# Attention and spiking feed-forward on one core: the last division through TensorE, later biases, and an order without random draws

## The chip, the core and the metric

One core of a Trainium2 chip runs the whole kernel in one launch. The metric is device microseconds of that core; lower is better. The engines are TensorE (PE, matrix products, with its weight loads shown apart as PEld), VectorE (DVE), ScalarE (ACT), GpSimd (POOL) and SyncE (SP, which issues nearly all DMAs here). Each engine takes its own instructions strictly in order, and waits on semaphores for the others.

## The reference, cut to what matters

The input x is [16, 1024, 256] in f32 (16 batches, 1024 tokens, 256 features). 16 heads have 16 features each; the feed-forward is 1024 wide.

```python
xn = layernorm(x)
Q, K, V = (xn @ W.T + b for each of q, k, v)        # split into 16 heads of 16
Q, K = rope(Q), rope(K)
scores = Q @ K.T / 4, causal mask
attn = softmax(scores) @ V                          # per head
a = concat(attn) @ Wo.T + bo
h = square(relu(xn @ W_fc.T)); y = h @ W_proj.T
f = number of spikes in 5 steps of a leaky neuron driven by y, over 5
out = x + a + f
```

## The kernel before, in words

**Units.** The attention works in 64 units: batch b, group g of four heads (`NG` = 4). For each unit `largest` (L785) first forms all causal scores (PE, L797) and takes each query's maximum on DVE (L813 for whole blocks, L831 for blocks on the diagonal). `placed` (L849) turns these maxima round on PE (L858), and SP writes them as two extra rows into the unit's query tile (L875). `weighted` (L904) then forms the scores again, transposed and with the maximum taken off by those rows (PE, L914), exponentiates them on ACT into "w" tiles (L975), masks the diagonal blocks on POOL (L932) and multiplies with the values (PE, L941, f32, four heads side by side in column quarters of the array). The values carry a column of constants beside each head's 16, so that the product has the sum of the exponentials in row 16 of each head's 32.

**The division.** Queries go in two halves `qb` of 512. When a half of a unit is done, its product is copied from PSUM to `avT` (L406, ACT, sometimes DVE at L412) and stored to DRAM (`av_dram`, L991). When two units (eight heads) are there, SP loads the sums (L1000) and the values (L1006) in a denser layout, DVE takes the reciprocals (L1014), SP stores them (L1017) and loads them spread over the 16 rows of each head (`inv`, `spread`, L949). POOL multiplies (L1023), ACT casts to f16 (L1025) and POOL keeps the remainder as a second f16 (L1028). These pairs of f16 are the `attn` tiles (128 rows for eight heads) that `projected` (L1033) multiplies with `wo_hi` and `wo_lo` (L599); DVE adds the product to the output tile (L1049) and SP stores that (L1052). A product in f32 precision from f16 parts is three f16 products (`three`, L596).

**Everything else.** `norms` (layer norm, transposes by DMA, L636), `rotated` (q and k with rope; on DVE in batch 0, on POOL in all others; stored to the DRAM scratch `scr`, L696 and L700), `values` (L738), and the feed-forward `forward` (L1072: `wfc` and `wproj` products at L599, L1106 to L1117 on ACT and POOL, the spikes on DVE at L1128). The x tile of the output is scaled on ACT (L1144) and gets the output bias `bo_sb` on POOL (L1146).

**The order.** All this is not issued as it is written. Each piece is an `op` with an engine, a cost, and a time `when` at which it is due; `Plan.order` (L199) plays the program through with these costs and writes the order in which each engine gets its instructions. An op may start up to a window (93 us of the plan's time unless given) before it is due, once what it reads is there and its tiles and PSUM banks are free. Buffers of one tag are handed out in turn: the next one waits until the oldest is free. The tag "w" has five buffers, "qkhl" (the f16 pairs of the rotated q and k) two. Each op's cost in that play is varied by up to 3% with a random generator whose seed is changed every 70 us of the plan; the seeds are the list `DRAWN` (L112 to L115, used at L273 to L276 and L328).

**The start.** `load_small` (L530) issues five DMAs on SP: wo in two parts, bv in two parts, bo. It is due at `SMALL` = -20 us of the plan, with a window of 10 us. From these come `wo_hi` and `wo_lo`, `bv_wide` (L550), a bias product on PE (L555) and the output bias (`biases`, L561).

```python
    op("sp", dma(5), SMALL, load_small, [], ["small", wo_stage], size=1400.0, window=10e3)
```

Of the kernel before, what the change touches and what calls it, by code (L numbers as in the profile page):

```python
# [4 lines left out]

# [1 line left out]

# [49 lines left out]
def least_values():  # L57
# [3 lines left out]
    for n in range(1, NUM_STEPS + 1):  # L61
        low, high = 0, int(np.float32(4 * THRESHOLD).view(np.int32))
        while high - low > 1:
# [3 lines left out]
            else:  # L67
# [22 lines left out]

BANKS = 8
AMONG = dict(pm="bm", ps="bs", ph="bf", py="bf", pqk="bf", pv="bf", po="bf", pav="ba",
             pnm="bo", pbo="bo")
CAPS = dict(bm=4, bs=4, bf=3, ba=2, bo=1)


# [8 lines left out]
SAME = dict(pe=0.0, act=60.0, dve=125.0, pool=100.0, sp=0.0)  # L105
S0 = -70e3
F0 = -22e3
SMALL = -20e3
L1, L2 = 30e3, 25e3
QD = 6.5e3  # L110

VARIED, STRETCH = 0.03, BATCH / 2  # L112
DRAWN = [
    0, 0, 1, 5, 3, 4, 6, 6, 4, 4, 7, 0, 0, 6, 0, 1, 7, 0, 4, 5, 6, 5, 5, 3, 7, 6, 0, 7, 2, 5, 1, 0, 2, 0,
]  # L115


class Held:
# [32 lines left out]
class Plan:  # L151
# [47 lines left out]
    def order(self):  # L199
# [17 lines left out]
        banks = [True] * BANKS  # L217
        rings = {}
        mode = None
        drawn, change, varied = list(DRAWN), -1e9, None  # L220

        def turn(t, need):

# [47 lines left out]

        while events:
            now = events[0][0]  # L273
            if now >= change:
                varied = Random(drawn.pop(0) if drawn else 0)
                change = S0 + STRETCH if change < S0 else change + STRETCH  # L276
            while events and events[0][0] <= now:
                _, _, kind, o = heappop(events)
                if kind == 0:
                    heappush(queues[o.engine], (o.when, o))  # L280
                    if o.alt:
                        heappush(events, (now + PATIENCE, n, 3, o))
                        n += 1
                elif kind == 3:
                    for engine, _, _ in o.alt:
                        heappush(spare[engine], (o.when, o))
                elif kind == 1:
                    busy[o.engine] = False
                    seen = now + SEEN[o.engine]
                    if o.size:  # L290
                        moved = max(moved, now + MOVE) + o.size
                        seen = moved + MOVED
                    for tile_ in o.held:
                        tile_.left -= 1
                        if not tile_.left:
                            heappush(events, (seen, n, 2, tile_))
                            n += 1
                    for p in o.then:
                        p.waits -= 1
                        same = p.engine == o.engine and not o.size  # L300
                        p.ready = max(p.ready, now + SAME[o.engine] if same else seen)
                        if not p.waits:
                            heappush(events, (max(p.ready, p.early), n, 0, p))
                            n += 1
                elif kind == 2:
                    for k in o.limits:
                        free[k] += 1
                    if isinstance(o, Held):
                        o.free = True
                    else:  # L310
                        banks[o.at] = True
            for engine in queues:
                if busy[engine]:
                    continue
                o = take(queues[engine])
                if o is None:
                    o = take(spare[engine])
                    if o is not None:
                        o.engine, o.cost, o.what = next(a for a in o.alt if a[0] == engine)
                if o is not None:  # L320
                    busy[engine] = True
                    o.start = now
                    order.append(o)
                    cost = o.cost
                    if engine == "pe":
                        cost += SWITCH * (o.mode != mode)
                        mode = o.mode
                    cost *= varied.uniform(1 - VARIED, 1 + VARIED)  # L328
                    heappush(events, (now + cost, n, 1, o))
                    n += 1  # L330
        assert len(order) == len(self.ops), "the plan does not get through"
# [13 lines left out]
def move(nbytes):  # L345
    return nbytes / 360.0


def dma(n):
    return 620.0 * n  # L350
# [6 lines left out]
def act(n):  # L357
    return 56 + 0.833 * n
# [11 lines left out]
def tile_block(ctx: ExitStack, tc, x, wqkv, bqk, bv, wo, bo, wfc, wproj, cos, sin, out):  # L370
# [52 lines left out]
    def held(tag, bufs, shape, dtype, name):  # L423
        return Held(sb, tag, BUFS.get(tag, bufs), shape, dtype, name)

    def load_x(b, n, tag, when):

        t = held(tag, 0, [P, 2, D], F32, f"{tag}_{b}_{n}")
        op("sp", 500, when, lambda: nc.sync.dma_start(t.t, tokens(x, b, n)), [], [t],
           size=move(P * 2 * D * 4))  # L430
        return t

    def tokens(a, b, n):
# [102 lines left out]
                bv_sb[:, k], bv[rows].rearrange("(h d o) -> d h o", d=DK, o=1))  # L536
        nc.sync.dma_start(bo_sb, bo.partition_broadcast(P))

    op("sp", dma(5), SMALL, load_small, [], ["small", wo_stage], size=1400.0, window=10e3)
    op("act", act(KD * D), SMALL + 1e3, lambda: nc.scalar.mul(wo_hi, wo_stage.t, WO_S),  # L540
       [wo_stage], [WO[0]])
    op("dve", dve(KD * D), SMALL + 1e3,
# [42 lines left out]
    class Batch:  # L585
        def __init__(self, b):
            self.b = b
            self.v = v_sb[b % 2]
            self.qS = []
            self.ready = []  # L590
            self.attn = [[None] * KD for _ in range(NQB)]
            self.av = [None] * NQB
            self.x = [None] * (NC // 2)
            self.xn = None
# [309 lines left out]
    def weighted(st, g, begin, end):  # L904
# [43 lines left out]
        def spread(qb, inv):  # L948
            nc.sync.dma_start(  # L949
                inv.t, inv_dram[qb].rearrange("(o h) q -> o h q", o=1).broadcast_to([DK, H // 2, QB])  # L950
            )


        steps = []
        for qb in range(NQB):
# [4 lines left out]
        for when, parts, n in zip(even(begin, end, widths), steps, widths):  # L960
# [25 lines left out]
            if last:  # L986
                avT = held("avT", 2, [P, QB], F32, f"avT_{unit}_{qb}")
                copied(QB, when + LAG + 1e3, lambda avT=avT: avT.t, lambda pav=pav: pav.t, [pav], [avT])
                home = av_dram[qb][unit // 2 % 2]
                op("sp", dma(1), when + LAG + 2e3,  # L990
                   lambda avT=avT, home=home: nc.sync.dma_start(  # L991
# [38 lines left out]
                       [*keys, (hl, 0)], [(hl, 1)])  # L1030


    def projected(st, times):  # L1033
        def product(c, po):
            qb, cc = divmod(c, CPB)
            for j in range(2):
                cols = slice((cc + j) * P, (cc + j + 1) * P)
                for k in range(KD):
                    hl = st.attn[qb][k]
                    three(  # L1040
                        po.t[:, j * D : (j + 1) * D],
                        [hl.t[:, part, cols] for part in range(2)],
                        [w[:, k, :] for w in w_o],
                        k == 0, k == KD - 1,
                    )

        def onto(n, po):
            xc = st.x[n].t.rearrange("p c d -> p (c d)")
            nc.vector.scalar_tensor_tensor(xc, xc, 1.0 / NUM_STEPS, po.t, ALU.mult, ALU.add)  # L1049

        def stored(n):
            nc.sync.dma_start(tokens(out, st.b, n), st.x[n].t)  # L1052

        for n in range(NC // 2):
            when = times[n]
            po = bank(f"po_{st.b}_{n}")
            keys = [
                (st.attn[2 * n // CPB][k], part) for k in range(KD) for part in range(2)
            ]
            op("pe", 12 * pe(D), when, lambda n=n, po=po: product(2 * n, po), [*keys, *WO], [po])  # L1060
            op("dve", dve(2 * D), when + 3e3, lambda n=n, po=po: onto(n, po), [po], [st.x[n]])
            op("sp", 500, when + 4e3, lambda n=n: stored(n), [st.x[n]], [],
               size=move(P * 2 * D * 4))
# [8 lines left out]
    def forward(st, times):  # L1072
# [62 lines left out]
        for t in range(S // T + 1):  # L1135
            for half in range(2):
                if t < S // T:
                    hTs[t, half] = hidden_ops(t, half, [times.pop(0) for _ in range(4)])
                if t > 0:
                    if half == 0:  # L1140
                        py = bank(f"py_{b}_{t - 1}")
                        st.x[t - 1] = x_ = load_x(b, t - 1, "x", times[0] - 15e3)
                        op("act", act(2 * D), times[0] - 8e3,
                           lambda x_=x_: nc.scalar.mul(x_.t, x_.t, float(NUM_STEPS)), [], [x_])  # L1144
                        op("pool", pool_(2 * D), times[0] - 6e3,
                           lambda x_=x_: nc.gpsimd.tensor_tensor(  # L1146
                               x_.t, x_.t,
                               bo_sb.rearrange("p (o d) -> p o d", o=1).broadcast_to([P, 2, D]),
                               ALU.add), ["bo"], [x_])
                    cc = half  # L1150
                    for part in range(2):
                        hT = hTs[t - 1, part]
                        for fs in (range(FH),):
                            when = times.pop(0)
                            times.pop(0)
                            op("pe", 3 * FH * pe(D), when,
                               lambda py=py, hT=hT, cc=cc, part=part, fs=fs: project(
                                   py, hT, cc, part, fs),
                               [(hT, 0), (hT, 1), *WPROJ], [py],
                               also=[st.x[t - 1]])  # L1160
                    if half == 1:
                        spikes(t - 1, py, when)
# [42 lines left out]
    for b in range(B):  # L1205
# [11 lines left out]
                   [st.ready[1]], [("kS", i)])  # L1217
        rotated(st, at["q", b])
        values(st, at["v", b])
        for g in range(NG):  # L1220
            t0 = b * BATCH + g * UNIT
            begin = t0 - UNIT - AHEAD
# [74 lines left out]
```

## Time and profile before

| What | Value |
|---|---|
| time of three runs | 2427.77 us median (2427.6 to 2428.23) |
| the profiled execution: time, span | 2432.1 us, 2430.4 us |
| granted TensorE clock, mean | 0.992 |
| core's 0 to 25.6 us: PE busy | 1.85 us |
| 25.6 to 80.7 us: PE, DVE busy | 44.13, 42.46 us |
| 2405.7 to 2430.4 us: PE busy, granted clock | 12.16 us, 0.67 |
| ACT, exponentials (L975) | 1246.4 us in 2560 instructions |
| POOL, masks (L932) | 398.0 us in 1024 |
| DMA, `av_dram` store, `sums` load, `inv` store, `inv` load: issue to landing | 2.5, 2.1, 1.8, 3.4 us (medians) |

The span is counted from the first to the last instruction of the profiled execution; the time of a run has a little around it. A busy share counts the time in which the engine had an instruction under way, and for PE it includes the time lost where the form of the array changes. A line of a group ends with the engine's idle time before those instructions and what released it.

### The profile page before, as it was taken

The numbers are of one execution on the slowest core, as the hardware profiler recorded it, in microseconds if no ns is written. First come the engines' busy times: TensorE is split into PE (matmuls) and PEld (weight loads), VectorE is DVE, ScalarE is ACT, GpSimd is POOL, SyncE is SP. The second block draws the span as 40 slices with busy tenths as digits, with TensorE's granted clock in tenths as the row PEclk, the third lists the DMA queues.
The fourth block names the chain that finished last, engine by engine and source line by source line (L and its number), as shares of the span: only waits on it lengthen the run. The fifth ranks groups of instructions, "written<-read, shape, count | busy, mean of one in ns | idle before, by whom it ended". The sixth has DMA issues, their size and how long they took to land. (4 is left out here: it accounts for less than half of the span.)

```text
span 2430.4 us, 58976 instructions
## 1 busy us (share of the span) xinstructions
PE 2344.1 (96%) x20996; PEld 1175.5 (48%) x20996; DVE 2000.4 (82%) x6070; ACT 1878.6 (77%) x3671; POOL 1769.9 (73%) x1897
## 2 busy tenths in 40 slices
PE   4999999999999999999999999999999999999997
PEld 2644444454455444454544445445454444545453
DVE  7788888888978888878888887988878888787982
ACT  5588788877877877878778877777877878778774
POOL 4878778777787787768768687676876858787453
PEclk9999999999999999999999999999999999999998
DMA  7443533524334243244342334333433343433221
GB/s 180 107 104 85 137 85 102 133 80 111 94 106 120 86 120 106 85 107 118 90 120 87 100 115 102 98 91 93 117 92 100 103 108 95 106 107 88 65 59 50
DMA packets 253936, 246.22 MB, mean 101 GB/s; under 512 B 108104, under 2 KB 207816, under 8 KB 253640
## 3 DMA queue, kind: packets, MB, share of 16 engines
q1 hardware_dynamic: 253504, 242.44, 36.4%
q8 instruction: 165, 2.70, 0.5%
q14 instruction: 131, 1.07, 0.2%
q10 hardware_dynamic: 136, 0.00, 0.0%
HBM read 122.82 MB, written 101.71 MB: 92 GB/s over the span
## 5 line engine op out<-in xcount | busy, mean ns | idle before, releaser
L975 ACT ACTIVATE w<-banks 128x512 f32<-128x512 f32 (+1 forms) x2560 | 1246.4, 573 | 285.3 <-PE banks L914 267.3
L813 DVE TENSOR_REDUCE nm_sb<-banks 128x1 f32<-128x512 f32 x1024 | 643.3, 682 | 138.8 <-PE banks L797 134.6
L941 PE MATMUL banks<-w,v_sb 128*32 128x512 f32 (+3 forms) x6144 | 620.7, 495 | 2.4 <-POOL w L932 0.4
L932 POOL TENSOR_SCALAR_AFFINE_SELECT w<-w 128x256 f32<-128x256 f32 x1024 | 398.0, 407 | 287.2 <-ACT w L975 275.1
L831 DVE CUSTOM_DVE_ANT_0 junk<-banks,mask,nm_sb 128x256 bf16<-128x256 f32 (+3 forms) x1024 | 498.7, 546 | 71.6 <-PE banks L797 40.2
L831 DVE CUSTOM_DVE_ANT_0 junk<-banks,mask 128x256 bf16<-128x256 f32 (+3 forms) x1024 | 444.6, 486 | 75.7 <-PE banks L797 60.3
L914 PE MATMUL banks<-qS,kS 50*128 50x512 f16 (+3 forms) x3072 | 430.5, 327 | 12.3 <-DVE nm_sb L831 7.6
L797 PE MATMUL banks<-kS,qS 48*128 48x512 f16 (+3 forms) x3072 | 420.6, 326 | 14.2 <-DVE nm_sb L831 5.4
L599 PE MATMUL banks<-wproj_hi,hT 128*128 128x256 f16 x2048 | 379.8, 274 | 1.1 <-DVE nm_sb L831 0.6
L599 PE MATMUL banks<-xT,wfc_hi 128*128 128x256 f16 x2048 | 353.5, 275 | 6.5 <-ACT qk L679 2.3
L599 PEld LDWEIGHTS <-hT 128*128 128x128 f16 x3072 | 281.0, 98 | 105.3 <-issue 73.7
L1113 POOL TENSOR_TENSOR relu<-relu 128x1024 f32<-128x1024 f32 x111 | 211.1, 1902 | 160.6 <-ACT hT L1111 160.3
L599 PE MATMUL banks<-xT,wfc_lo 128*128 128x256 f16 x1024 | 280.4, 274 | 0.0
L599 PE MATMUL banks<-wproj_lo,hT 128*128 128x256 f16 x1024 | 279.4, 273 | 0.0
L1117 POOL TENSOR_TENSOR hT<-relu,hT 128x1024 f16<-128x1024 f32 x128 | 274.1, 2141 | 3.6 <-ACT relu L1115 1.7
L914 PEld LDWEIGHTS <-kS 50*128 50x128 f16 x3072 | 132.9, 94 | 296.3 <-issue 269.1
L797 PEld LDWEIGHTS <-qS 48*128 48x128 f16 x3072 | 138.7, 94 | 277.7 <-issue 236.1
L941 PEld LDWEIGHTS banks<-w,v_sb 128*32 128x32 f32 x6144 | 151.6, 108 | 250.8 <-issue 195.3
L1128 DVE SCALAR_TENSOR_TENSOR x<-banks,x 128x512 f32<-128x512 f32 x320 | 219.0, 684 | 46.0 <-PE banks L599 39.1
L1106 ACT ACTIVATE relu<-banks 128x512 f32<-128x512 f32 x256 | 156.3, 611 | 121.6 <-PE banks L599 118.2
L599 PEld LDWEIGHTS <-wfc_hi 128*128 128x128 f16 x2048 | 184.6, 98 | 95.2 <-issue 72.7
L686 POOL TENSOR_TENSOR ms<-qk,sin_sb 128x1024 f32<-128x1024 f32 x60 | 142.0, 2367 | 47.6 <-ACT qk L679 47.6
(81 smaller groups left out, 2798.5 us busy)
## 6 DMA issues: line engine op xcount, KB each, us to landing
av_dram<-avT SPq DMA_DIRECT2D x128, 256.0 KB, 2.5
qS<-scr_q SPq DMA_DIRECT2D x128, 192.0 KB, 3.6
kS<-scr_k SPq DMA_DIRECT2D x128, 192.0 KB, 4.4
x<-in_x_dram SPq DMA_DIRECT2D x66, 256.0 KB, 3.7
scr_q<-qkhl SPq DMA_DIRECT2D x32, 512.0 KB, 3.1
scr_k<-qkhl SPq DMA_DIRECT2D x32, 512.0 KB, 3.1
av<-av_dram SPq DMA_DIRECT2D x64, 256.0 KB, 3.4
inv<-inv SPq DMA_DIRECT2D x64, 256.0 KB, 3.4
```

The source lines that it names most:

```text
L599: nc.tensor.matmul(out, lhsT=lhs[i], rhs=rhs[j], start=first and n == 0, stop=last and n == 2)
L797: nc.tensor.matmul(pts[two].t[:, at : at + w], lhsT=qS.t[r, h, c * P : (c + 1) * P], rhs=kS[r, h, k0 : k0 + w], start=True, stop=True,)
L813: lambda two=two, pt=pt: nc.vector.tensor_reduce(nm0[:, two, i, c : c + 1], pt.t, axis=AX.X, op=ALU.max),
L831: nc.vector.tensor_tensor_reduce(next(junk)[:, :w], pt.t[:, at : at + w], mask[:, QB - w :], scale=1.0, scalar=nm0[:, two, i, chunk] if pa ...
L914: nc.tensor.matmul(pts[two].t[:, at : at + n], lhsT=kS[r, i, j * P : (j + 1) * P], rhs=qS.t[r, i, qb * QB + off : (qb + 1) * QB], start=Tr ...
L932: nc.gpsimd.affine_select(out=d, in_=d, compare_op=ALU.is_ge, fill=0.0, base=0, pattern=[[0, 2], [1, P]], channel_multiplier=-1,)
L941: nc.tensor.matmul(pav.t[VT * h : VT * (h + 1), off:], lhsT=st.v[:, j, col : col + VT], rhs=ws[h % 2].t[:, h // 2, at : at + QB - off], st ...
L975: lambda n=n, two=two, pt=pt, w=w: nc.scalar.activation(w.t[:, two, :n], pt.t[:, :n], AF.Exp, scale=SCALE),
L1106: lambda r=r, ph=ph, pr=pr: nc.scalar.activation(r.t[:, 2 * pr : 2 * pr + 2].rearrange("p f t -> p (f t)"), ph.t, AF.Relu, scale=1.0 / WS),
L1113: combined(1024, when + 4e3, lambda e, r=r: e.tensor_tensor(r.t, r.t, r.t, ALU.mult), [], [(r, 0), (r, 1)], 1.75, lambda r=r: nc.scalar.ac ...
L1117: lambda e, r=r, hT=hT: e.tensor_tensor(hT.t[:, 1], r.t, hT.t[:, 0], ALU.subtract),
L1128: nc.vector.scalar_tensor_tensor(xc, py.t, WS * LEAST[step], xc, ALU.is_gt, ALU.add)
```

## The change

Three things are changed.

1. The random variation of costs in `Plan.order` is taken out: `DRAWN`, `VARIED`, `STRETCH` and the import are gone, and every op has its plain cost.
2. `SMALL` goes from -20e3 to 32e3 ns of the plan, and the cost of its loads from `dma(5)` = 3100 to 5000 ns. The x loads of batch 0 get a shorter window, so that they do not come long before the bias that is added to them.
3. For the last batch's second half of queries, the last two groups (`ending`) no longer go through DRAM. `inverted` takes the sums out of `avT` by a product with columns of the identity, inverts them, widens each over 32 columns, turns them back by a second product, and multiplies `avT` with the result. Each of the two groups then has an f16 pair of its own, in the layout with 32 rows a head, and needs the rows of wo in that layout: `load_slots_of_wo` loads them with eight DMAs into a "w" buffer, and ACT and DVE turn them into an f16 pair in a "qkhl" buffer, after the last rotated q and k of the batch have been stored. The last two output products have three parts instead of two.

```diff
-SMALL = -20e3
+SMALL = 32e3
...
-                    cost *= varied.uniform(1 - VARIED, 1 + VARIED)
...
-    op("sp", dma(5), SMALL, load_small, [], ["small", wo_stage], size=1400.0, window=10e3)
+    op("sp", 5e3, SMALL, load_small, [], ["small", wo_stage], size=1400.0, window=10e3)
...
+        def inverted(st, g, avT, when):
+            ps, pi = bank(f"psum_{unit}"), bank(f"pinv_{unit}")
+            inv = held("sums", 2, [P, CPB, 4], F32, f"sums_{unit}")
+            wide = held("av", 2, [P, CPB, 4, VT], F32, f"av_{unit}")
+            st.slots[g] = hl = held("ahl", 5, [P, 2, QB], F16, f"ahl_{unit}")
+            def columns():
+                for c in range(CPB):
+                    nc.tensor.matmul(
+                        ps.t[:, 4 * c : 4 * (c + 1)], lhsT=avT.t[:, c * P : (c + 1) * P],
+                        rhs=ident32.rearrange("p (h v) -> p h v", v=VT)[:, :, DK],
+                        start=True, stop=True,
+                    )
+            def spread_out():
+                nc.vector.reciprocal(inv.t.rearrange("p c h -> p (c h)"), ps.t[:, : 4 * CPB])
+                nc.vector.tensor_copy(
+                    wide.t.rearrange("p c h v -> p (c h) v"),
+                    inv.t.rearrange("p c (h o) -> p (c h) o", o=1).broadcast_to([P, 4 * CPB, VT]),
+                )
+            def rows():
+                for c in range(CPB):
+                    nc.tensor.matmul(
+                        pi.t[:, c * P : (c + 1) * P],
+                        lhsT=wide.t[:, c].rearrange("p h v -> p (h v)"), rhs=ident32,
+                        start=True, stop=True,
+                    )
+            op("pe", 600, when, columns, [avT], [ps])
+            op("dve", 700, when + 0.5e3, spread_out, [ps], [inv, wide])
+            op("pe", 900, when + 1e3, rows, [wide], [pi])
+            op("dve", dve(QB), when + 2e3,
+               lambda: nc.vector.tensor_tensor(avT.t, avT.t, pi.t, ALU.mult), [pi], [avT])
+            op("act", act(QB), when + 3e3, lambda: nc.scalar.copy(hl.t[:, 0], avT.t),
+               [avT], [(hl, 0)])
+            op("dve", dve(QB), when + 4e3,
+               lambda: nc.vector.tensor_tensor(hl.t[:, 1], avT.t, hl.t[:, 0], ALU.subtract),
+               [avT, (hl, 0)], [(hl, 1)])
...
+                if ending(st.b, g, qb):
+                    inverted(st, g, avT, when + LAG + 2e3)
+                    continue
...
+    def ending(b, g, qb):
+        return b == B - 1 and g >= NG - 2 and qb == NQB - 1
+    def load_slots_of_wo(when):
+        slots = held("qkhl", 2, [P, 2, 2, D], F16, "wo_slots")
+        stage = held("w", 4, [P, 2, D], F32, "wo_slots_stage")
+        def load():
+            for i in range(2):
+                for h in range(4):
+                    row = ((NG - 2 + i) * 4 + h) * DK
+                    nc.sync.dma_start(stage.t[VT * h : VT * h + DK, i], wo[row : row + DK])
+        op("pool", 1000, when, lambda: nc.gpsimd.memset(stage.t, 0.0), [], [stage], window=10e3)
+        op("sp", dma(8), when + 1e3, load, [], [stage], size=800.0)
+        op("act", act(2 * D), when + 3e3, lambda: nc.scalar.mul(slots.t[:, 0], stage.t, WO_S),
+           [stage, *[("scr", (B - 1) % 2, t, 1) for t in range(2)]], [slots])
+        op("dve", dve(2 * D), when + 4e3,
+           lambda: nc.vector.scalar_tensor_tensor(
+               slots.t[:, 1], stage.t, WO_S, slots.t[:, 0], ALU.mult, ALU.subtract),
+           [stage], [slots])
+        return slots
...
+        if b == B - 1:
+            wo_slots = load_slots_of_wo(b * BATCH)
```

The new products `columns` and `rows` take their PSUM banks from the same quota as those of the turned maxima.

## The prediction

> **What bounds the kernel now.** I read the busy shares first, then stretches of the span, then the costliest groups, then the first 30 us and the last 25 us in order of time.
>
> ```profile
> span 2430.4 us, 58976 instructions
> PE 2344.1 (96%) x20996; PEld 1175.5 (48%) x20996; DVE 2000.4 (82%) x6070; ACT 1878.6 (77%) x3671; POOL 1769.9 (73%) x1897
> ...
> PEclk9999999999999999999999999999999999999998
> ...
> L975 ACT ACTIVATE w<-banks 128x512 f32<-128x512 f32 (+1 forms) x2560 | 1246.4, 573 | 285.3 <-PE banks L914 267.3
> L813 DVE TENSOR_REDUCE nm_sb<-banks 128x1 f32<-128x512 f32 x1024 | 643.3, 682 | 138.8 <-PE banks L797 134.6
> ...
> L831 DVE CUSTOM_DVE_ANT_0 junk<-banks,mask,nm_sb 128x256 bf16<-128x256 f32 (+3 forms) x1024 | 498.7, 546 | 71.6 <-PE banks L797 40.2
> L831 DVE CUSTOM_DVE_ANT_0 junk<-banks,mask 128x256 bf16<-128x256 f32 (+3 forms) x1024 | 444.6, 486 | 75.7 <-PE banks L797 60.3
> ```
>
> TensorE (PE) is the bound: it idles 86 us in 2430. VectorE (DVE) and ScalarE (ACT) are not far below, and their largest work comes per unit (4 heads of one batch; 64 units): the maxima cost DVE (643.3 + 498.7 + 444.6) / 64 = 24.8 us a unit, the exponentials ACT 1246.4 / 64 = 19.5 us.
>
> ```profile
> 395.50:2137.70 1742.20, 1712.07 (x15459) 850.08 (x15460) 1458.37 (x4479) 1378.74 (x2707) 1307.31 (x1405) 1.00 0.37 103
> 2137.70:2173.70 36.00, 35.78 (x340) 17.62 (x334) 30.84 (x107) 28.39 (x56) 32.04 (x35) 1.00 0.33 98
> 2173.70:2282.10 108.40, 107.41 (x998) 55.02 (x996) 89.23 (x274) 82.90 (x164) 69.87 (x80) 1.00 0.31 89
> 2282.10:2405.70 123.60, 121.36 (x1109) 59.17 (x1108) 87.62 (x247) 94.86 (x191) 63.05 (x84) 0.99 0.19 55
> ```
>
> These stretches (start:end, length, then busy us of PE, weight loads, DVE, ACT, POOL) are cut at units 8, 56, 57, 60 and at the last score of unit 63. PE idles 30.1 us in the 1742 of the middle and 3.6 us in the 268.0 of the last eight units: feed-forward products still fill PE there.
>
> ```profile
> 8.79 0.60 SPq L534 DMA_DIRECT2D wo_stage<-in_wo_dram  x1
> ...
> 19.55 0.35 SPq L537 DMA_DIRECT2D bo_sb<-in_bo_dram  x1
> ...
> 21.53 1.37 SPq L636 DMA_TRANSPOSE xT<-xhl  x1
> ...
> 2408.03 0.58 ACT L406 COPY avT<-banks 128x512 f32<-128x512 f32 x1 [1.30 <-PE banks L941]
> ...
> 2415.67 0.52 SPq L949 DMA_DIRECT2D inv<-inv  x1
> 2419.09 1.26 POOL L1023 TENSOR_TENSOR av<-av,inv 128x512 f32<-128x512 f32 x1 [8.72 <-DMA inv<-inv]
> ...
> 2426.56 0.69 DVE L1049 SCALAR_TENSOR_TENSOR x<-x,banks 128x512 f32<-128x512 f32 x1 [1.87 <-PE banks L599]
> ```
>
> At the start the bias loads hold SP's queue from 8.79 to 19.9 us, and the first transpose goes out behind them, though its input was written at 14.6. At the end the last sums go out to DRAM and back: 13 us from the copy (2408.03) to the first product that uses them (2421.06).
>
> **A measure of PE work.** The order of instructions on each engine is fixed when a program is built and can be read in both programs. Twelve 256-column f16 products take 1.42 us up to the next tile form in the chain of waits; their columns alone are 1.28 (0.107 each), so a change of form (whole array, row halves, column quarters) costs about 0.15. I price every product by columns so (512-column score pairs 0.213, four quarter products in f32 0.853) and every change at 0.15. The middle stretch then has 1718 us against 1712 busy, so the measure holds.
>
> **The draws go: another order everywhere.** Up to unit 56 the old order has 2097 changes of form, the new one 2052: 45 x 0.15 = -7 us. Feed-forward products left at unit 56 are 732 in both, and the PE work between a unit step's scores and the product that uses them is alike (median 3.7 us in both), so I take the idle of the middle as unchanged. Its bounds: the calmest 300 us of the page's span idle 2.0 us, the worst 9.2; over 1742 us that is 12 or 53 instead of 30, so -18 to +23.
>
> **Biases later.** The five loads leave the head of SP's queue for the place behind the wproj and x loads. The transpose can follow its input: 21.5 - 14.7 = -6.8 us for the rotation on DVE, which DVE works through without a gap (34.5 to 66.7) and which sets when the first maxima can start (80.7). Given back: bv_wide, wo_lo and the two bias operations (0.29 + 0.69 + 0.7 = 1.7 us by their rows) now stand among the rotations on DVE. DVE there, and PE behind it, may also wait for the bv load, whose two DMAs took 12.6 us to land; behind PE's wait stand feed-forward products with slack before the first maxima, behind DVE's the rotations. I take 1 us. So -4, between -7 and +3 (7 us of wait). POOL's additions of bo move behind, where they have room.
>
> **The slots of wo.** By themselves eight DMA issues (0.6 us each on SP, 5 us in front of an inv store), one memset, one ACT and one DVE operation are hidden under PE. But the staging tile takes one of the five "w" buffers, which otherwise carry exponentials and are handed out in turn. The memset is placed in unit 56, and the conversions that free the buffer wait for the last rotation store of batch 15, since the result sits in a "qkhl" buffer. The new order shows what this does: on ACT 33 operations without an exponential stand between two of unit 56; on PE no score stands in 48.8 us of work by the measure, where 228 feed-forward products, 72 of the projections and the maxima of 1.4 units are pulled forward. That leaves nothing to fill with later: after the last feed-forward product come 124 of the 48 x 64 scores (before: 26). Priced by stretch of scores, new against old:
> - unit 56: 80.2 us of PE work. POOL has 65 by its rows (rotations 2.37, 1.28 and 2.14, squares 1.90, remainders 2.14), 48 of them in the part without scores, against the same on PE; two chains that feed each other. With the last eight units' ratio of busy to measure (264.4 / 258.1 = 1.025) 82, plus 5 for the coupling: 87 (82 to 92).
> - units 57, 58: 56.0 x 1.025 = 57.4, plus 2: 59 (57 to 64).
> - units 59 to 62: PE 108.8 x 1.025 = 111.5, but DVE 115 (maxima 4 x 24.8 and other rows). DVE becomes the bound; at 95% 121 (115 to 128). The max rows of units 62 and 63 have 3.5 us of PE work to hide in, where the median is 6.6 and their way (0.6 DVE, 2.5 of issues, 1.7 landing) takes 5: 1.5 us each, in this range.
> - unit 63: ACT 19.5 + 1.2 + 1.6 = 22 (21 to 24), now 22.6.
>
> Together 289 against 268.0: +21, between +7 and +40.
>
> **The division through PE.** Removed: three DMA waits. Added, from the copied avT (2408.6): four f32 column products with 128-column weights. Nearest rows: f32 weight loads 0.108 (32 columns) and 0.34 (L555, at half clock), two to a product, so 0.9 to 2.9, taken 1.5. Reciprocal and wide copy 0.25 + 0.65 (rows: 128x32 0.35, 128x512 0.66). Four 128x128 f32 products, 0.21 to 0.5 each plus loads: 1.6 to 4.7, taken 2.5. Multiply 0.69, cast 0.62, remainder 0.68, six handovers 0.6. In all 7.5, so 2416.1 instead of 2422.3. On PE 60 output products (12 more than now, since the slots need three parts and not two) stand behind both, from 2413.7. In the trace products after gaps of 0.81 and 0.84 us ran at 0.21 us until 2413.9, 3.5 us long, then at 0.107. So 16 at 0.21 and 44 at 0.107: 2421.9, where it is 2426.5 now: -4.5. Bounds: cheap ends at full clock -8; dear ends, all at 0.215, +3.
>
> The Trainium skill ("TensorE: Matmul & The Clock Gate", Part 1: The HAM clock gate) puts the fall to half rate behind an idle window of about 3.4 us. The gaps here would not reach that, all 60 products would run at full rate, and the end would be an estimated 1.7 us earlier; the trace's own half-rate products after gaps of 0.8 us speak against it, and I keep 0.21.
>
> **Sum.** 2430.4 - 7 - 4 + 21 - 4.5 = 2435.9 as a span. The median lies 2.6 below this span (2427.8), so 2433.3; with the DVE-bound stretch likelier long than short I say 2434.
>
> **Rivals.**
> - The window without scores is free (faster). PE's work is only reordered, the ends of the ranges hold (+7 where I have +21): 2420. For it: PE, POOL and DVE have work throughout; the old tail ran ACT gapless for 8.1 us. Against it: DVE would have to run at 100% for four units, where its best 10 us here are 89%. It decides once the last eight units stay under 278 us.
> - The draws had earned something. The middle idles as its worst 300 us: +23, 2457. For it: order affects idle by a factor of four between stretches. Against: fewer changes of form and like distances in the new order.
> - The end does not pay: half clock to the last product and dear f32 products, +3 instead of -4.5: 2441. For it: the clock is 0.50 in the last 10 us now. Against: 60 products in a row are over three times the 3.5 us after which it rose.
>
> **How the numbers follow.** Forecast 0.46 (2425 to 2445), no cost 0.22, draws 0.20, end 0.12. A measurement of this kernel tells 0.2% (4.9 us) from no change, so the borders are 2422.9 and 2432.6. Slower: 0.46 x 0.58 + 0.20 + 0.10 = 0.57. Within: 0.46 x 0.40 + 0.06 = 0.25. Faster: 0.18 from the first rival. The range from 2416 to 2454 leaves out the better part of the first rival's and the worse part of the second's.
>
> **What will show it.** Right, if around unit 56 (near 2125 to 2210 us) ACT has some 50 us without exponentials and PE stays nearly full, if PE idles 15 us or more in the last 75 us before the end with DVE above 90% first and ACT after, if the first transpose goes out near 15 us, and if the copied sums reach the last products in 7 to 9 us. Wrong, if PE's idle in the middle moves by over 10 us, or if the last eight units take under 278.

## The result, and the profile after

| | median of the runs | span of the profiled execution |
|---|---|---|
| before (4 runs beside the changed kernel) | 2428.0 us (2427.6 to 2433.61) | 2430.4 us |
| after (4 runs) | 2446.68 us (2445.98 to 2450.13) | 2444.2 us |
| ratio after / before | 1.0072, 95% interval 1.0056 to 1.0087 | |

The change makes the kernel 0.7% slower, 18.7 us by the medians. The forecast was 2434: the direction held and the time lies in the range, but the loss is three times the forecast's.

The spans differ by 13.8 us only. The profiled execution of before took 2432.1 us, 4.3 more than the median of its first three runs; that of after took 2445.98, which is typical for it. About 5 us of the 18.7 are therefore in no comparison of the two traces.

The page of the changed kernel, busy shares and the two costliest groups that were shown of before:

```profile
span 2444.2 us, 59065 instructions
PE 2357.7 (96%) x21040; PEld 1188.3 (49%) x21040; DVE 1988.5 (81%) x6077; ACT 1877.5 (77%) x3672; POOL 1772.1 (73%) x1898
...
PEclk9999999999999999999999999999999999999998
...
L1007 ACT ACTIVATE w<-banks 128x512 f32<-128x512 f32 (+1 forms) x2560 | 1246.4, 578 | 273.0 <-PE banks L904 256.1
L803 DVE TENSOR_REDUCE nm_sb<-banks 128x1 f32<-128x512 f32 x1024 | 642.1, 682 | 149.0 <-PE banks L787 147.2
```

The exponentials (now L1007) and the maxima (L803) cost what they did. PE is busy 13.6 us longer (2357.7 against 2344.1) and idles the same 86 us. The page's averages do not show where that comes from, so I cut the span into stretches, in both kernels by the same rule: a unit ends on PE with the last of its scores in the program's order, matched one by one to the trace. The columns are start:end, length, then busy us of PE, weight loads, DVE, ACT and POOL, the granted clock, DMA share and GB/s. First before, from unit 8, cut at units 56, 57, 59, 63 and at the last score:

```profile
396.10:2142.80 1746.70, 1716.57 (x15498) 852.15 (x15499) 1461.76 (x4494) 1383.01 (x2716) 1311.34 (x1409) 1.00 0.37 103
2142.80:2173.80 31.00, 30.78 (x300) 15.29 (x300) 26.98 (x87) 23.57 (x48) 27.51 (x28) 1.00 0.38 113
2173.80:2244.10 70.30, 69.80 (x646) 34.99 (x644) 53.73 (x154) 58.43 (x114) 51.89 (x57) 1.00 0.33 100
2244.10:2378.90 134.80, 134.17 (x1255) 68.68 (x1254) 118.39 (x360) 98.16 (x198) 71.05 (x90) 1.00 0.22 61
2378.90:2405.80 26.90, 24.80 (x206) 10.52 (x204) 4.62 (x8) 21.23 (x45) 9.99 (x18) 0.94 0.14 42
2405.80:2430.40 24.60, 12.06 (x74) 6.98 (x72) 3.01 (x5) 2.66 (x7) 5.86 (x7) 0.67 0.24 77
```

The same stretches of after:

```profile
381.60:2134.70 1753.10, 1721.09 (x15592) 865.30 (x15591) 1449.02 (x4489) 1386.93 (x2722) 1336.17 (x1421) 1.00 0.39 103
2134.70:2217.20 82.50, 80.09 (x683) 48.25 (x683) 59.95 (x167) 50.16 (x86) 63.82 (x48) 1.00 0.28 83
2217.20:2272.90 55.70, 55.52 (x532) 26.91 (x531) 35.94 (x116) 46.90 (x96) 32.53 (x45) 1.00 0.29 74
2272.90:2400.00 127.10, 118.46 (x1061) 52.80 (x1060) 108.44 (x331) 91.52 (x186) 54.20 (x81) 0.97 0.23 63
2400.00:2424.10 24.10, 22.10 (x165) 7.95 (x163) 3.10 (x6) 19.73 (x45) 6.80 (x18) 0.93 0.13 36
2424.10:2444.20 20.10, 13.82 (x101) 10.25 (x100) 4.92 (x8) 2.60 (x7) 3.39 (x5) 0.79 0.16 53
```

Up to unit 56 the changed kernel is 8.1 us ahead (2134.7 against 2142.8). The last eight units take 289.4 us instead of 263.0, +26.4. What follows the last score is 4.5 shorter (20.1 against 24.6). The sum is +13.8, the difference of the spans.

Of the +26.4, only 9.8 are PE's idle time (13.2 us against 3.4); PE is also busy 16.6 us longer (276.2 against 259.6). That is not more work: the columns and changes of form of its products in the last eight units, priced as in the prediction, come to 260.0 us against 257.6. The busy time that grew lies in units 59 to 63. Products come there one or two at a time, and a product that has none behind it counts as busy for longer (one score of 512 columns 0.37 us, two together 0.38); and the clock is at half for 10.2 us of the last eight units instead of 3.4.

In the last eight units PE first works nearly without a pause (unit 56, 80.09 of 82.50 us, but for 82 us instead of 31), and then idles where before it did not: 8.6 us in units 59 to 62 (127.10 - 118.46) against 0.6. There the clock is granted at 0.97 instead of 1.00 as well.

That unit 56 does other work than its own is seen on ACT. The exponentials alone, ten us at a time (start:end, length, busy and count, clock, DMA share, GB/s):

```profile
2140.00:2150.00 10.00, 4.28 (x11) 1.00 0.57 177
2150.00:2160.00 10.00, 2.36 (x5) 1.00 0.28 82
2160.00:2170.00 10.00, 0.00 (x0) 1.00 0.27 86
2170.00:2180.00 10.00, 0.00 (x0) 1.00 0.14 48
2180.00:2190.00 10.00, 0.00 (x0) 1.00 0.35 107
2190.00:2200.00 10.00, 0.00 (x0) 1.00 0.25 82
2200.00:2210.00 10.00, 5.49 (x11) 1.00 0.00 1
```

The last exponential ends at 2153.2 and the next begins at 2203.4: 50 us without one. The staging tile's own instructions show why (median duration and count, then first and last start in us):

```profile
L1079 SPq DMA_DIRECT2D wo_slots_stage<-in_wo_dram x8: 406/418/539, 2145.0 to 2148.3; - x8
L1081 POOL MEMSET wo_slots_stage<- x1: 524/524/524, 2144.4 to 2144.4; 128x512 f32 x1
L1084 ACT ACTIVATE wo_slots<-wo_slots_stage x1: 612/612/612, 2199.9 to 2199.9; 128x512 f16<-128x512 f32 x1
L1087 DVE SCALAR_TENSOR_TENSOR wo_slots<-wo_slots_stage,wo_slots x1: 1666/1666/1666, 2200.6 to 2200.6; 128x512 f16<-128x512 f32 x1
```

The tile is filled by about 2151 and read at 2199.9, after the last store of rotated k has gone out (L690 at 2195.9). From 2144.4 to 2202.3 one of the five "w" buffers is held, and since they are handed out in turn, the exponentials stop when its turn comes.

The start and the end of the span, in order of time (start, length, engine, line, instruction, and in brackets the idle time before it and its releaser):

```profile
14.00 0.66 DVE L648 TENSOR_TENSOR xhl<-xn,xhl 128x512 f16<-128x512 f32 x1
14.69 1.36 SPq L626 DMA_TRANSPOSE xT<-xhl  x1
...
27.27 0.62 SPq L523 DMA_DIRECT2D wo_stage<-in_wo_dram  x1
...
2426.28 0.58 ACT L395 COPY avT<-banks 128x512 f32<-128x512 f32 x1 [1.30 <-PE banks L931]
2426.92 1.06 PE L953 MATMUL banks<-ident,avT 128*128 128x4 f32 x8 [0.72 <-ACT avT L395]
...
2428.96 2.08 PE L968 MATMUL banks<-ident,av 128*128 128x128 f32 x8 [0.98 <-DVE av L961]
2431.14 0.69 DVE L978 TENSOR_TENSOR avT<-avT,banks 128x512 f32<-128x512 f32 x1 [2.24 <-PE banks L968]
...
2432.51 0.69 DVE L982 TENSOR_TENSOR ahl<-avT,ahl 128x512 f16<-128x512 f32 x1 [0.69 <-ACT ahl L979]
```

The first transpose goes out at 14.69 instead of 21.53. At the end the copied sums (2426.86) become the finished pair at 2433.20, 6.3 us, without a DMA.

### The profile page after: what moved, and what is told of

The parts are those of the page before. It is cut to its first block, busy times and chain, and to the rows that moved or that the text cites. A ratio compares the mean times of both kernels' runs of the same rounds, so it can differ in the third digit from the quotient of the medians.

```text
span 2444.2 us, 59065 instructions
## 1 busy us (share of the span) xinstructions
PE 2357.7 (96%) x21040; PEld 1188.3 (49%) x21040; DVE 1988.5 (81%) x6077; ACT 1877.5 (77%) x3672; POOL 1772.1 (73%) x1898
## 3 DMA queue, kind: packets, MB, share of 16 engines
q14 instruction: 130, 1.06, 0.2%
## 5 line engine op out<-in xcount | busy, mean ns | idle before, releaser
L1007 ACT ACTIVATE w<-banks 128x512 f32<-128x512 f32 (+1 forms) x2560 | 1246.4, 578 | 273.0 <-PE banks L904 256.1
L803 DVE TENSOR_REDUCE nm_sb<-banks 128x1 f32<-128x512 f32 x1024 | 642.1, 682 | 149.0 <-PE banks L787 147.2
L904 PE MATMUL banks<-qS,kS 50*128 50x512 f16 (+3 forms) x3072 | 436.6, 328 | 11.0 <-DVE nm_sb L821 4.9
```

What stands on the lines that cost most here:

```text
L803: lambda two=two, pt=pt: nc.vector.tensor_reduce(nm0[:, two, i, c : c + 1], pt.t, axis=AX.X, op=ALU.max),
L904: nc.tensor.matmul(pts[two].t[:, at : at + n], lhsT=kS[r, i, j * P : (j + 1) * P], rhs=qS.t[r, i, qb * QB + off : (qb + 1) * QB], start=Tr ...
L1007: lambda n=n, two=two, pt=pt, w=w: nc.scalar.activation(w.t[:, two, :n], pt.t[:, :n], AF.Exp, scale=SCALE),
```

## The experiments

A time is a median with the lowest and highest run; a ratio is taken to runs of the kernel before on the same chip (2429.43 us over 23 runs for e1 to e4; 2431.68 over 24 for e5 to e8). "PE idle of units 8 to 55" is summed from the gaps in the trace that are longer than 0.15 us (with the shorter ones it is 30.1 us before, 1746.70 - 1716.57, and 32.0 in the changed kernel). The changed kernel itself was timed beside 2428.0, so a difference of medians between two of these groups can be off by the 1.4 to 3.7 us by which the kernel before differs between them.

### e1: the draws alone are taken out

```diff
-                    cost *= varied.uniform(1 - VARIED, 1 + VARIED)
```

> The kernel before with only the random variation of costs taken out; biases and division as before. Theory (the held w buffer is the cause): the draws cost or gain little, so within 8 us of the kernel before (2428), and no gap without scores. Rival (the draws had placed the work well and their loss is the cause): 10 to 20 us slower than before, near the changed kernel's 2447.

Measured 2438.78 us (2437.78 to 2440.55), ratio 1.0042 (1.0027 to 1.0056): +9.4, a little more than the expectation allowed. PE idle of units 8 to 55 is 33.8 us against 23.7 before. But the loss is not there: PE is busy 9.9 us less in these units (1706.7 against 1716.6), and unit 56 begins at 2142.0 (before: 2142.8). Units 56 to 63 then take 270.9 us instead of 263.0, and the end 25.1 instead of 24.6. On the old start and end the plain order is the worse one, in the last eight units.

### e2: no draws and later biases, division as before

The changed kernel without its third part: `inverted`, `load_slots_of_wo` and the three-part products are out.

```diff
-SMALL = -20e3
+SMALL = 32e3
...
-                    cost *= varied.uniform(1 - VARIED, 1 + VARIED)
```

> The kernel before without draws and with the biases loaded later, but with the division of all groups through DRAM. Its order on TensorE is that of the changed kernel up to unit 56, then without the 48.8 us without scores. Theory (held w buffer): the start of unit 56 as in the changed kernel (2135 us), the last eight units about 266 instead of 289, the end 24.6 as before: span 2426, time about 2427, some 20 below the changed kernel. Rival (draws): 2440 or more.

Measured 2431.34 us (2428.59 to 2436.89), ratio 1.0011 (1.0 to 1.0022): 4 us above what was expected, 7.5 below e1 and 15.3 below the changed kernel. Up to unit 56 its instructions on PE stand in the changed kernel's order, and unit 56 begins at 2134.3 (after: 2134.7). Units 56 to 63 then take 267.8 us instead of 289.4. So nothing before unit 56 makes the changed kernel slow; what was added there does. Most of the 4 us above the expectation lie in the end, 27.8 us instead of 24.6: the granted clock is 0.50 from 2410.2 to the end of the span.

### e3: the staging tile leaves the ring

The changed kernel whole, with the staging tile in a buffer of the tag "xn", which is free in the last batch.

```diff
-        stage = held("w", 4, [P, 2, D], F32, "wo_slots_stage")
+        stage = held("xn", 0, [P, 2, D], F32, "wo_slots_stage")
```

> The changed kernel with the staging tile of the wo slots in an xn buffer (free by then) instead of a w buffer; nothing else. Order as in the changed kernel up to unit 56. Theory (held w buffer): the gap without scores goes, the last eight units take about 266 instead of 289, the end stays at 20 us: span 2422, time about 2424, so 23 below the changed kernel and 4 below the kernel before. Rival (draws): no more than 5 below the changed kernel, 2441 or more.

Measured 2423.61 us (2420.8 to 2431.96), ratio 0.9978 (0.9967 to 0.9989): 23.1 below the changed kernel, and below the kernel before. The stretches of e3, units 56, 57 to 58, 59 to 62 and 63:

```profile
2137.20:2171.00 33.80, 33.38 (x306) 15.91 (x305) 29.36 (x96) 25.73 (x52) 25.59 (x26) 1.00 0.42 117
2171.00:2244.20 73.20, 72.33 (x662) 36.52 (x660) 58.31 (x171) 58.46 (x113) 56.86 (x61) 1.00 0.32 96
2244.20:2381.50 137.30, 136.52 (x1275) 70.31 (x1274) 116.83 (x345) 100.24 (x199) 70.52 (x91) 1.00 0.21 58
2381.50:2405.90 24.40, 22.82 (x198) 9.57 (x196) 5.87 (x10) 19.70 (x43) 9.11 (x18) 1.00 0.11 35
```

and its conversion of the staging tile:

```profile
L1084 ACT ACTIVATE wo_slots<-wo_slots_stage x1: 699/699/699, 2237.3 to 2237.3; 128x512 f16<-128x512 f32 x1
```

Memset, loads, conversion and the wait for the last store are all still there; the tile is even held longer, from 2146.9 to 2240. But it is no buffer of the ring, unit 56 takes 33.8 us, and PE idles 0.8 in units 59 to 62.

### e4: a held buffer alone, in the kernel before

To the kernel before one "w" buffer is added that is filled in the last batch and scaled after the last rotation store. Nothing uses it; it adds one POOL and one ACT instruction.

```diff
+    def hold(when):
+        stage = held("w", 4, [P, 2, D], F32, "hold")
+        op("pool", 1000, when, lambda: nc.gpsimd.memset(stage.t, 0.0), [], [stage], window=10e3)
+        op("act", act(2 * D), when + 3e3, lambda: nc.scalar.mul(stage.t, stage.t, 1.0),
+           [("scr", (B - 1) % 2, t, 1) for t in range(2)], [stage])
```

> The kernel before, draws and all, with one w buffer taken by a memset in the last batch and held until the batch's rotated q and k are stored, then scaled in place by ScalarE; nothing uses it. Order as before up to unit 56, then a gap of 42.8 us of TensorE work without scores. Theory (held w buffer): 20 to 26 us slower than before, 2448 to 2454, with the last two units short of feed-forward products. Rival (draws): within 3 us of before, as the draws are still there.

Measured 2450.84 us (2441.07 to 2453.88), ratio 1.0085 (1.0065 to 1.0105): +21.4, as expected. Its stretches, cut as above:

```profile
2143.00:2174.00 31.00, 30.78 (x296) 15.31 (x294) 26.96 (x87) 23.60 (x47) 27.45 (x28) 1.00 0.39 113
2174.00:2275.40 101.40, 100.77 (x884) 55.92 (x882) 68.76 (x199) 69.81 (x130) 71.48 (x67) 1.00 0.25 72
2275.40:2398.90 123.50, 117.88 (x1076) 54.84 (x1075) 105.59 (x319) 90.57 (x186) 54.71 (x81) 1.00 0.23 64
2398.90:2424.30 25.40, 22.31 (x149) 5.66 (x148) 0.81 (x3) 19.84 (x44) 6.54 (x17) 0.80 0.16 45
```

Before unit 57 nothing moves. Units 57 and 58 grow from 70.3 to 101.4 us with PE full, and units 59 to 62 have PE idle for 5.6 us. It is the changed kernel's picture one unit later. The built program agrees: after the last feed-forward product come 116 scores, in the changed kernel 124, before 26, in e3 32.

### e5: the buffer stays in the ring, but for a short time

The changed kernel with the slots in a buffer of the tag "xhl", so that the conversion need not wait for the stores.

```diff
-        slots = held("qkhl", 2, [P, 2, 2, D], F16, "wo_slots")
+        slots = held("xhl", 2, [P, 2, 2, D], F16, "wo_slots")
...
-           [stage, *[("scr", (B - 1) % 2, t, 1) for t in range(2)]], [slots])
+           [stage], [slots])
```

> The changed kernel with the staging tile still in a w buffer, but the wo slots in an xhl buffer (free by then), so that their conversion does not wait for the last rotated q and k and gives the w buffer back at once. Theory (it is the long hold): as with the staging tile elsewhere, 2424 within 5 us, no gap without scores. Rival (a w buffer taken out of turn costs by itself, or the eight loads and conversions do): 2432 or more.

Measured 2422.59 us (2418.88 to 2429.06), ratio 0.9961 (0.9947 to 0.9975). The "w" buffer is taken at 2141.7 and read by ACT at once:

```profile
L1081 POOL MEMSET wo_slots_stage<- x1: 525/525/525, 2141.7 to 2141.7; 128x512 f32 x1
L1084 ACT ACTIVATE wo_slots<-wo_slots_stage x1: 700/700/700, 2150.4 to 2150.4; 128x512 f16<-128x512 f32 x1
L1087 DVE SCALAR_TENSOR_TENSOR wo_slots<-wo_slots_stage,wo_slots x1: 690/690/690, 2152.1 to 2152.1; 128x512 f16<-128x512 f32 x1
```

It is held for 11 us instead of 58, and units 56 to 63 take 268.8 us. Neither the ring alone nor the wait alone costs anything (e5, e3); both together cost 23. The end is 16.3 us long in this execution, the fastest of e5's runs, against 20.1 in the changed kernel: the clock stays at 1.00, where the changed kernel has 0.50 for 6.7 us from 2429.0, and the output products begin 3.1 us after the copy of the last product, where they begin 5.0 after it in the changed kernel.

### e6 and e7: draws again, on e3

e3 with the variation of costs: e6 with the old list of seeds, e7 with seeds 8 to 41.

```diff
+                    cost *= varied.uniform(1 - VARIED, 1 + VARIED)
```

> The kernel with the staging tile in an xn buffer, and the old list of draws put back. Theory A (the draws suit only the order they were found with; on another they are one more order): 2424 within 10 us. Theory B (varied costs help as such): 9 us below 2423.6, as much as their loss cost the kernel before, so 2415.

> As the run before, with another list of draws (seeds 8 to 41). Theory A: 2424 within 10 us, and not equal to the run with the old list. Theory B: near 2415 like it.

e6 measured 2434.16 us (2430.4 to 2437.29), ratio 1.0013 (1.0003 to 1.0023), e7 2423.84 us (2422.22 to 2426.76), ratio 0.9968 (0.9957 to 0.998). With later biases and the new division the old list is 10.5 us worse than no draws (8.5 by the two ratios, since e3 ran on another chip), where with the old start and end it was 9.4 better (e1). Another list is as good as none. PE idle of units 8 to 55 is 29.9 in e6 and 18.7 in e7, but e7 loses in units 0 to 7 (285.9 us from the first score that feeds an exponential; after 271.0). A list is worth something for one program only; what shifts is which order comes out, by about 10 us either way.

### e8: the division alone

The kernel before, draws and early biases kept, with the division through TensorE and the staging tile in "xn".

```diff
+        stage = held("xn", 0, [P, 2, D], F32, "wo_slots_stage")
...
+                if ending(st.b, g, qb):
+                    inverted(st, g, avT, when + LAG + 2e3)
+                    continue
```

> The kernel before with its draws and its early biases, and only the division of the last two groups through TensorE added, its staging tile in an xn buffer. Order as before up to unit 56. Theory (the division is worth the 4.5 us that the end of the trace shows): 2429.4 - 4.5 = 2425, the stretch after the last score 20 us. Rival (the step from 2431.3 to 2423.6 between two earlier runs is all division): 2429.4 - 7.7 = 2421.7.

Measured 2430.9 us (2427.35 to 2436.38), ratio 0.9996 (0.9987 to 1.0006): -1.0 +- 2.4 us, less than the 4.5 expected. What follows the last score is 20.2 us long, 4.4 shorter than before, as the prediction has it. But the orders of the two programs, which agree up to unit 56, differ after it, and unit 63 takes 30.1 us instead of 27.0; which row of that order costs the 3 us was not tried. (The profiled execution is the slowest of e8's runs, 2436.38, and 4.5 us late when unit 56 begins, where the orders are still the same; from there on it takes 0.2 us less than the kernel before.) By the medians of e3 and e2, on the other order, the division earns 7.7, and their traces show this at the end too: 27.8 us in e2, 19.3 in e3. So the end earned 4.4 us here and 8.5 there, and the clock takes part in that: it is granted at 0.50 for 19.7 of the 27.8 us in e2, and at 0.67 on average in the 24.6 us before.

### The account

| step | runs | us |
|---|---|---|
| draws out | e1 - before | +9.4 |
| biases later | e2 - e1 | -7.5 |
| division through TensorE, no buffer of the ring held | e3 - e2 | -7.7 |
| the staging tile in the ring, held over the stores | after - e3 | +23.1 |
| sum | | +17.3 |

The measured 18.7 is 1.4 more, because the kernel before had 2429.43 beside e1 to e3 and 2428.0 beside the changed kernel. The first three rows hold for this order of the steps: e6 and e8 show other prices for draws and division on other orders.

Without the last row the change is 0.2 to 0.4% faster than the kernel before (e3, e5), and 1.0% faster than the kernel as changed (2422.59 / 2446.68 = 0.990).

## Why the prediction was right, and where it was off

**The mechanism: right, and shown.** The prediction has the staging tile take one of the five "w" buffers, which "are handed out in turn", and hold it until the last rotation store: e3 and e5 take away the one and the other half of it and get 23 and 24 us back, e4 adds it alone and loses 21. Of the signs named beforehand, ACT's 50 us without exponentials came (2153.2 to 2203.4), the first transpose near 15 us came (14.69), and DVE was full before the end (10.00 busy of the ten us from 2360, 9.96 of those from 2370). One sign was badly chosen: PE idles 12.4 us in the last 75 where "15 us or more" were named, and before it idled 14.7 there.

**The pieces of the last eight units: their sum right, the subtraction wrong.** The prediction had 87 + 59 + 121 + 22 = 289 us, measured 82.5 + 55.7 + 127.1 + 24.1 = 289.4. From this it took the 268.0 of before. The new pieces were cut in the program's order, but the 268.0 began at 2137.7 in the trace, where only 2684 of the 2688 scores of units 0 to 55 had been made; the last came at 2142.1. By one ruler the old eight units are 263.0 long, and the step is +26, not +21. This is one of the two steps that failed most, by 5.0 us (the other is the one from span to median, below), and no run was needed to find it: the same cut on both sides. The ratio of busy to measure, 264.4 / 258.1 = 1.025, has the same fault: the 258.1 are the work behind the last score of unit 55 (257.6 by the trace at the same prices), and the busy time from there on is 259.6. By one ruler the ratio is 1.006, and the pieces priced with it were some 2% too dear on that account.

**Within the pieces.** Unit 56 did not need the 5 us "for the coupling" of PE and POOL: PE is busy 80.09 of 82.50. In units 59 to 62 DVE was to become the bound, "at 95%"; DVE is busy 85% of them (108.44 of 127.10), and only from 2360 to 2380 full. PE and DVE take turns in waiting there, and after PE's pauses its clock is at half for 6.8 us (last section), which costs it up to 3.4: 127 instead of 121. The misses cancel (-4.5, -3.3, +6.1, +2.1); that the sum came out right is luck.

**Up to unit 56: -8.1 instead of -11.** The 45 fewer changes of form are there (2052 against 2097, -6.8 at 0.15). The first product on PE comes 5.9 us earlier (17.9 against 23.8). PE's gaps up to unit 56 grow by 3.0 us in all (41.9 against 38.9), and 1.6 lie in products that are slower than their columns and changes. The idle of units 8 to 55 is 26.2 against 23.7, inside the bounds of -18 to +23 around "unchanged". By the runs the two steps do not split as the prediction had them. Taking the draws out is no gain of 7 by itself but a loss of 9.4 (e1, on the old start and end), and the bias step is worth -7.5 (e2 - e1) against -4 taken, just past its bound of -7; its other bound adds up to +2, not +3 (-6.8 + 1.7 + 7).

**The end: -4.5, as predicted.** The sums took 6.3 us instead of 7.5, but the end does not wait for the finished pair: other output products stand in front of those that use it. These begin 5.0 us after the copy, 5.1 in the prediction, because two misses cancel: the f32 products are cheaper (1.06 and 2.08 us instead of 1.5 and 2.5), and PE then waits 0.85 us for the multiplication (L978). They ran at half rate somewhat longer (4.0 us instead of 3.5). Neither comes with every end: in e5 there is no such wait and no half rate, and the end takes 16.3 us. That -4.5 was met so closely is in part luck.

**From span to median: the other 5.1 us.** "The median lies 2.6 below this span" was read from one execution of before that was 4.3 us slow for its kernel. In after the median lies 2.5 above the span. With 5.0 from the ruler, 2.9 from the stretch up to unit 56 and 0.4 from the pieces, this is the 13.4 us between 2433.3 and 2446.7.

**The rivals.** "The window without scores is free" is refuted: the last eight units stay over 278 us, and e3 without the window is 23 us faster. The argument brought against it had a wrong reading, though: DVE's best ten us in the kernel before are not at 89% but full (10.00 busy from 2126). "The draws had earned something" is true by itself (e1: +9.4), though not by the idle time of the middle that it named, since the loss is in the last eight units; and yet it is not the cause here: in the changed kernel's order taking them out is no loss (e6 is slower with them). "The end does not pay" is refuted by the trace; by the medians its worth depends on what order comes with it and on the clock at the end (e8 -1.0, e3 - e2 -7.7).

## What to carry to other kernels

Before a setup step borrows a buffer from a ring that is handed out in turn, ask when the last reader of it can run: the ring stops behind it for as long as it is held, however cheap the step is. Work pulled forward into the hole isn't lost by itself, but it is then missing as filler at the end, where the other engines set the pace; so look at what is left to fill with after the hole. And cut both kernels by the same rule before you subtract, and don't take one profiled execution for the median.

## What the runs showed of the hardware

**Short pauses can bring the TensorE clock down.** In the starved stretch of after, PE's own rows (start, length, line, tiles, count, idle before):

```profile
2372.63 0.28 PE L904 MATMUL banks<-qS,kS 50*128 50x256 f16 x2 [0.51 <-ACT w L1007]
...
2375.89 0.37 PE L787 MATMUL banks<-kS,qS 48*128 48x512 f16 x1 [0.76 <-DVE nm_sb L821]
2376.50 0.37 PE L787 MATMUL banks<-kS,qS 48*128 48x512 f16 x1 [0.24 <-DVE nm_sb L821]
...
2377.72 0.61 PE L787 MATMUL banks<-kS,qS 48*128 48x512 f16 x2 [0.22 <-DVE nm_sb L821]
```

The two scores of 512 columns from 2377.72 on take 0.61 us; at full clock two such took 0.38 in the same kernel (2136.34). No pause before them is longer than 0.8 us. In the 3.4 us from 2374.3 PE is busy for 2.18 us and the granted clock is still 1.00; in the 6.7 us from 2377.8 it is 0.50. At the end it is the same: in the 3.4 us from 2425.5 PE is busy for 1.75 us, with pauses of 0.72 and 0.98 us, and from 2429.0 on the clock is 0.50; the 256-column products come every 0.21 us from 2431.88 to 2435.8, then every 0.107. Short pauses do not always do it: in e5 the same two pauses (0.72 and 0.99 us) leave the clock at 1.00 to the end of the span. No run varied the pauses alone, so how much of them it takes stays open. The Trainium skill ("TensorE: Matmul & The Clock Gate", Part 1: The HAM clock gate) has the gate close after an idle window of about 3.4 us and open after as long of work; the opening agrees (4.0 us here), the closing, as it is put there, does not: the runs show it after pauses of under 1 us that follow each other.

**Small products in f32.** Four 128x128 f32 products with four columns take 1.06 us (L953, granted clock 1.00). With 128 columns they take 2.08 us here (L968), at a granted clock of 0.50, and 1.16 us in e5, at 1.00. The prediction had 1.5 and 2.5.

**A change of tile form** costs about 0.15 us (0.136 to 0.158 in every stretch of both kernels where PE is not starved); by the two forms that meet the medians lie between 0.11 and 0.15 us.
